# A two-layer decoder in one kernel: softmax probabilities of two attentions transposed by VectorE squares and DRAM instead of by TensorE

## The chip, the core and the metric

The kernel runs on one core of a Trainium2 chip. The core has a matrix engine (TensorE, in the profile PE, with its weight loads as PEld), a vector engine (VectorE, DVE), an activation engine (ScalarE, ACT), a general engine (GpSimd, POOL) and a queue that issues transfers (SyncE, SP). Matrix products are written to PSUM, eight banks of 128 x 512 float32; the other data are in SBUF, 128 partitions wide. The engines run side by side, each through its own list of instructions in order, and wait for each other by semaphores.

The metric is the device time of one execution in microseconds, as the median of several runs.

## What is computed

The input is x, 16 blocks of 128 tokens by 512, and a context, 16 blocks of 128 by 128. All is float32. Two layers, each with an attention, a second attention to the context, and a feed-forward part; after each of the six parts, `x = layernorm(x + part(x))`:

```python
x = _layernorm(x + _L0_attn_ref(x, ...))     # 16 heads of 32, 4 key heads, additive mask, softmax
x = _layernorm(x + _L0_xattn_ref(x, ctx, ...))  # 16 heads, keys from the context, softmax
x = _layernorm(x + _L0_ffn_ref(x, ...))      # ternary weights
x = _layernorm(x + _L1_attn_ref(x, ...))     # linear attention with decay, no softmax
x = _layernorm(x + _L1_xattn_ref(x, ctx, ...))  # 16 heads of 32, causal, softmax
x = _layernorm(x + _L1_ffn_ref(x, ...))      # mixture of 8 experts, 2 chosen, and a shared one
```

The change touches mainly the first and the fifth part. The core of both is, for each block of 128 tokens and each of 16 heads:

```python
scores = einsum("qd,kd->qk", q, k) * scale + mask    # 128 x 128
p = softmax(scores, axis=-1)
out = einsum("qk,kd->qd", p, v)                      # then all heads through an output projection
```

## The kernel before, in words

The program is written with a framework that builds the lists of the engines at compile time: a scheduler orders the instructions by priority (roughly, the order in which they are written) and by when it thinks that each is ready, and sets the semaphores. `tc.keep_in_program_order` takes an instruction out of that freedom: it stays in the written order on its engine.

The two attentions with 16 heads (called first and second attention here; lines 254 to 450 with `p1`, and 880 to 943 with `p5`) share a function, `attend`. It goes over 16 blocks `n` and 2 more turns, so that three blocks are in flight:

- **Scores** of block n: 16 small products on TensorE (L444, L931) into four PSUM banks of tag `sc`, four heads in each.
- **Softmax** in four parts `c` of four heads. `start` (L182): add the mask on VectorE into an SBUF tile `t` (L184), the row maximum on VectorE (L186), four exponentials on ScalarE with their sums (L191). `finish`, one part later: the reciprocal on VectorE (L197), a multiplication on GpSimd (L198).
- **Turn** of block n-1 (L200): the value product needs the probabilities with the keys on the partitions. `turn` transposes the four heads of a part on TensorE, by a product with the identity (L203), into a PSUM bank of tag `pt`, and VectorE copies the bank to an SBUF tile `pT` (L205).
- **Values** of block n-2: products into one `pt` bank (L450, L938), evicted by ScalarE to `oT` (L246), then `project_out` (L148, bank of tag `mm`), whose result VectorE adds to x (L149); a layer norm follows, with its last step on GpSimd (L121).
- **Preparation** of the next group of four blocks: `Share.deal` hands out, in parts between the softmax parts, the transposes of x (L127, bank `mm`, evicted by ScalarE at L128), the projections for queries, keys and values (L137 and, in the first attention, L422; bank `mm`). In the first attention the folds are dealt too: weights for the next part are multiplied together (`fold`, L283 to L307, bank `mm`), from raw weights of 1728 KB per fold, loaded by SP with two buffers (L389).

PSUM's eight banks in both attentions: 2 `mm`, 4 `sc`, 2 `pt`. A float32 product appears as two records in the profile; a transpose appears as one.

The second part (the attention to the context with wide heads, `p2`, L504 to L650) has a class `Heads` that already turns its probabilities in another way: VectorE transposes the 32 x 32 squares of a 128 x 128 matrix in place (L580), a transfer writes the result to a DRAM tile `away` (L584), and four transfers read it back with the squares moved to their places (L587). Its PSUM: 2 `mm`, 4 `sc`, 2 `av`.

The last part needs two DRAM arrays, `slots_x` and `sums`, set to zero. SP does that with two transfers of 10 MB each (L891), issued as the second attention prepares its first group, together with the loads of the shared expert's weights.

## Time and profile before

| | us |
|---|---|
| median of 3 runs | 2102.04 (2098.30 to 2102.48) |
| the profiled execution, its time | 2102.39 |
| the profiled execution, its span | 2100.6 |
| TensorE busy in the span | 2038.5 (97%) |
| VectorE busy | 853.1 (41%) |
| ScalarE busy | 625.0 (30%) |
| GpSimd busy | 646.8 (31%) |
| mean busy share of the DMA engines over the span | about 35% |
| first attention, from first score to last projection | 34.4 to 260.9 |
| second attention, likewise | 1311.5 to 1519.3 |

The span is what the engines' records cover; the execution's own time is 1.8 us longer. The profile's columns are busy times: TensorE's products are pipelined, and their ends are modelled, so a busy TensorE is not one at its peak. In the groups of instructions a line reads: line, engine, operation, output<-input, shape, count | busy us, mean ns of one | idle us of the engine before them, and what ended most of it.

### The profile page before, as it was taken

The numbers are of one execution on the slowest core, as the hardware profiler recorded it, in microseconds if no ns is written. First come the engines' busy times: TensorE is split into PE (matmuls) and PEld (weight loads), VectorE is DVE, ScalarE is ACT, GpSimd is POOL, SyncE is SP. The second block draws the span as 40 slices with busy tenths as digits, with TensorE's granted clock in tenths as the row PEclk, the third lists the DMA queues.
The fourth block names the chain that finished last, engine by engine and source line by source line (L and its number), as shares of the span: only waits on it lengthen the run. The fifth ranks groups of instructions, "written<-read, shape, count | busy, mean of one in ns | idle before, by whom it ended". The sixth has DMA issues, their size and how long they took to land. (4 is left out here: it accounts for less than half of the span.)

```text
span 2100.6 us, 25187 instructions
## 1 busy us (share of the span) xinstructions
PE 2038.5 (97%) x9221; PEld 1125.7 (54%) x9221; DVE 853.1 (41%) x1728; ACT 625.0 (30%) x2103; POOL 646.8 (31%) x674
## 2 busy tenths in 40 slices
PE   8999989999999999999999999999899999999997
PEld 5555544444444458888555444555544455545552
DVE  4667732444554243222123213777731122232324
ACT  3655532333333222222211111766632200000002
POOL 5555530111211122223223123455613212222223
PEclk9999999999999999999999999999999999999999
DMA  6001231334432220000300008600003379999974
GB/s 230 1 35 40 106 129 54 99 124 125 136 119 78 70 85 1 1 1 35 120 1 1 1 6 248 244 22 21 26 19 126 122 218 305 295 295 305 289 236 165
DMA packets 117067, 238.19 MB, mean 113 GB/s; under 512 B 28752, under 2 KB 73168, under 8 KB 110288
## 3 DMA queue, kind: packets, MB, share of 16 engines
q1 hardware_dynamic: 102048, 129.72, 19.1%
q0 software_dynamic: 13792, 105.55, 15.3%
q8 instruction: 73, 1.20, 0.2%
q10 hardware_dynamic: 1104, 1.31, 0.2%
q14 instruction: 50, 0.41, 0.1%
HBM read 172.25 MB, written 64.30 MB: 113 GB/s over the span
## 5 line engine op out<-in xcount | busy, mean ns | idle before, releaser
L198 POOL TENSOR_TENSOR p<-p,rs 128x512 f32<-128x512 f32 x192 | 200.0, 1043 | 504.8 <-DVE rs L197 500.0
L605 PE MATMUL po<-mT,cc 128*128 128x512 f32 x512 | 232.5, 602 | 3.7 <-ACT cc L598 3.7
L191 ACT ACTIVATE p<-t,nmx 128x128 f32<-128x128 f32 x512 | 198.5, 390 | 34.6 <-POOL p L198 8.8
L605 PEld LDWEIGHTS po<-mT,cc 128*128 128x128 f32 x512 | 95.5, 191 | 117.7 <-issue 107.4
L191 ACT ACTIVATE p<-sc,nmx 128x128 f32<-128x128 f32 x256 | 90.0, 372 | 113.7 <-DVE nmx L186 107.9
L546 PE MATMUL pq<-xT,wqr 128*128 128x512 f32 x256 | 117.9, 602 | 3.0 <-ACT xT L128 3.0
L114 POOL TENSOR_SCALAR ve<-mv 128x1 f32<-128x1 f32 x80 | 18.1, 226 | 324.3 <-DVE mv L112 312.3
L148 PE MATMUL po<-wo,oT 128*128 128x512 f32 x256 | 116.8, 599 | 0.4 <-ACT qkT L414 0.4
L1163 ACT ACTIVATE rsg<-rg 128x352 f32<-128x352 f32 x39 | 18.1, 463 | 331.2 <-PE rg L1158 331.2
L775 PE MATMUL pq<-xT,wq 128*128 128x512 f32 x256 | 110.9, 594 | 1.0 <-ACT xT L128 0.7
L1158 PE MATMUL rg<-ew,xsT 128*128 128x352 f32 x312 | 100.5, 465 | 11.3 <-DMA ew<-in_l1f_w_dram,which 10.6
L1179 PE MATMUL ry<-ew,ractT 128*128 128x512 f32 (+1 forms) x234 | 106.9, 592 | 0.0
L121 POOL TENSOR_SCALAR x<-x,mv,rstd 128x512 f32<-128x512 f32 x48 | 100.6, 2095 | 4.5
L1158 PE MATMUL ru<-ew,xsT 128*128 128x352 f32 x312 | 98.7, 459 | 0.0
L1129 POOL DMA_INDIRECT ew<-in_l1f_w_dram,which x39 | 38.0, 975 | 190.7 <-PE ry L1179 167.9
L191 ACT ACTIVATION_READ_ACCUMULATOR p<-t,nmx 128x1 f32 x512 | 96.2, 188 | 0.0
L698 POOL TENSOR_TENSOR hl<-ht,hh 128x512 fp32r<-128x512 f32 x44 | 60.4, 1372 | 114.9 <-ACT hh L696 114.9
L205 DVE COPY pT<-pt 128x512 f32<-128x512 f32 x128 | 86.5, 679 | 18.0 <-PE pt L203 18.0
L1189 POOL DMA_INDIRECT sums<-ry,place x39 | 62.0, 1590 | 96.2 <-DMA sums<-ry,place 43.9
L203 PEld LDWEIGHTS pt<-ident,p 128*128 128x128 f32 x512 | 59.8, 141 | 53.8 <-issue 44.8
L1041 PE MATMUL pg<-xT,sw_gu 128*128 128x512 f32 x192 | 86.5, 593 | 0.0
L186 DVE TENSOR_REDUCE nmx<-t 128x4 f32<-128x512 f32 x128 | 83.8, 675 | 0.8
(231 smaller groups left out, 3617.7 us busy)
## 6 DMA issues: line engine op xcount, KB each, us to landing
piece<-in_l0f_w_dram SPq DMA_DIRECT2D x48, 352.0 KB
away<-sq SPq DMA_DIRECT2D x32, 512.0 KB
pT<-away SPq DMA_DIRECT2D x128, 128.0 KB
raw<-in_l0x_raw_dram SPq DMA_DIRECT2D x8, 1728.0 KB
slots_x<-zero SPq DMA_DIRECT2D x1, 10023.0 KB
sums<-zero SPq DMA_DIRECT2D x1, 9984.0 KB
xs<-slots_x SPq DMA_DIRECT2D x156, 64.0 KB
sums<-x SPq DMA_DIRECT2D x16, 256.0 KB
```

Of the source, the lines that this page charges most:

```text
L121: engine.tensor_scalar(x[b], x[b], mean, rstd, ALU.subtract, ALU.mult)
L148: nc.tensor.matmul(po, lhsT=oT[:, c, :], rhs=wo[:, c, :], start=(c == 0), stop=(c == KC - 1))
L186: nc.vector.tensor_reduce(nmx, src, axis=AX.X, op=ALU.max, negate=True)
L191: nc.scalar.activation(self.p[:, j, :], src[:, j, :], AF.Exp, bias=nmx[:, j : j + 1], accum_out=self.sm[:, j : j + 1])
L198: nc.gpsimd.tensor_tensor(self.p, self.p, spread(rs, P), ALU.mult)
L205: nc.vector.tensor_copy(self.pT, pt)
L546: nc.tensor.matmul(pq, lhsT=wqr[:, k, cols], rhs=xT[:, k, :], start=(k == 0), stop=(k == KC - 1))
L605: nc.tensor.matmul(self.po, lhsT=self.cc[:, 4 * par + j, :], rhs=mT[h], start=(par == 0 and j == 0), stop=(par == 1 and j == 3),)
L775: nc.tensor.matmul(pq, lhsT=wq4[k // 2][:, k % 2, c * P : (c + 1) * P], rhs=xT[:, k, :], start=(k == 0), stop=(k == KC - 1))
L1041: nc.tensor.matmul(dst, lhsT=sw_gu[:, k, at : at + P], rhs=xTs[g][:, k, :], start=(k == 0), stop=(k == KC - 1),)
L1158: nc.tensor.matmul(dst, lhsT=self.xT[:, k, :], rhs=gu[:, k, off : off + FE], start=(k == 0), stop=(k == KC - 1),)
L1179: nc.tensor.matmul(po, lhsT=self.actT[:mw, m_, :], rhs=dn[:mw, m_, :], start=(m_ == 0), stop=(m_ == 2))
```

## The change

- The turn of the probabilities. `turn` is gone. A class `Turn` transposes the 32 x 32 squares on VectorE into a tile `sq` of half a block (two parts), sends each half to DRAM (`away`, 512 KB), and after the second half reads the block back with four transfers into one tile `pT` of 1 MB, of which there is one buffer. The last block of each attention is still turned on TensorE (`here`), through `mm` banks.
- The order. A class `Order` keeps the instructions that go through it in the written order: TensorE's, VectorE's and ScalarE's of the softmax, the squares, the eviction of `oT`, and the addition to x. `attend` is rewritten around four slots a block: values of block n-2 before slot 1, their projection in slot 2, the addition and the layer norm in slot 3, a part of the preparation in slots 0, 1 and 3; the squares of a part come two slots after its `start`. One turn fewer follows the last block.
- The masked scores are written into the tile `p` itself instead of into a tile `t`, and the exponentials are computed in place.
- PSUM. Both attentions: 2 `mm`, 5 `sc`, 1 `pt`. The second part (`p2`): 4 `mm`, 2 `sc`, 2 `av`.
- The zero fills of `slots_x` and `sums` are issued in the feed-forward stage of the first layer, before its second group.

The diff, cut to its core:

```diff
-    psum.share(mm=2, sc=4, pt=2)
+    psum.share(mm=2, sc=5, pt=1)
...
+    class Order:
+        kept = False
+        def one(self, instruction):
+            if self.kept:
+                tc.keep_in_program_order(instruction)
+        def matmul(self, *args, **kw):
+            self.one(nc.tensor.matmul(*args, **kw))
+        def transpose(self, *args):
+            self.one(nc.tensor.transpose(*args))
+    te = Order()
...
-    def project_out(oT, wo, b):
+    def project_out(oT, wo):
         po = bank("mm", [P, D], "po")
         for c in range(KC):
-            nc.tensor.matmul(po, lhsT=oT[:, c, :], rhs=wo[:, c, :], start=(c == 0), stop=(c == KC - 1))
-        nc.vector.tensor_tensor(x[b], x[b], po, ALU.add)
+            te.matmul(po, lhsT=oT[:, c, :], rhs=wo[:, c, :], start=(c == 0), stop=(c == KC - 1))
+        return po
+    def add_norm(b, po):
+        te.one(nc.vector.tensor_tensor(x[b], x[b], po, ALU.add))
         layernorm(b, nc.gpsimd)
...
             if self.mask is not None:
-                src = self.pool.tile([P, 4, P], F32, tag="t", name="t", bufs=3)
-                nc.vector.tensor_tensor(src, self.sc, bc(self.mask, 4), ALU.add)
+                src = self.p
+                te.one(nc.vector.tensor_tensor(src, self.sc, bc(self.mask, 4), ALU.add))
...
-        def turn(self):
-            pt = bank("pt", [P, 4, P], "pt")
-            for j in range(4):
-                nc.tensor.transpose(pt[:, j, :], self.p[:, j, :], ident)
-            self.pT = self.pool.tile([P, 4, P], F32, tag="pT", name="pT", bufs=4)
-            nc.vector.tensor_copy(self.pT, pt)
+    class Turn:
+        def __init__(self, pool):
+            self.pool = pool
+            self.away = dram.tile([P, 4, 2, 8 * Q], F32, tag="away", name="away", bufs=2)
+        def squares(self, c, p):
+            if c % 2 == 0:
+                self.sq = self.pool.tile([P, 4, 8, Q], F32, tag="sq", name="sq", bufs=2)
+            at = slice(c % 2 * 4, c % 2 * 4 + 4)
+            te.one(nc.vector.transpose(
+                self.sq[:, :, at, :].rearrange("p k h q -> p h k q"), p.rearrange("p h (k a) -> p h k a", a=Q)
+            ))
+            if c % 2:
+                nc.sync.dma_start(self.away[:, :, c // 2, :], self.sq.rearrange("p k h q -> p k (h q)"))
+            if c == 3:
+                self.back()
+        def here(self, ps):
+            self.pT = self.pool.tile([P, 4, 16, Q], F32, tag="pT", name="pT", bufs=1)
+            for c, p in enumerate(ps):
+                pt = bank("mm", [P, 4, P], "pt")
+                for j in range(4):
+                    te.transpose(pt[:, j, :], p[:, j, :], ident)
+                nc.vector.tensor_copy(
+                    self.pT[:, :, 4 * c : 4 * c + 4, :].rearrange("p t h q -> p h t q"),
+                    pt.rearrange("p h (t q) -> p h t q", q=Q),
+                )
+            return self
+        def back(self):
+            self.pT = self.pool.tile([P, 4, 16, Q], F32, tag="pT", name="pT", bufs=1)
+            rows = self.away.rearrange("(t a) k n f -> k a t (n f)", a=Q)
+            for k in range(4):
+                nc.sync.dma_start(self.pT[k * Q : (k + 1) * Q].rearrange("a t h q -> a t (h q)"), rows[k])
...
+        te.kept = True
+        def values(n):
+            av = bank("pt", [P, KC, P], "av")
+            held.pop(n)
+            value(av, n, turns.pop(n).pT)
+            oT = pool.tile([P, KC, P], F32, tag="oT", name="oT")
+            te.one(nc.scalar.copy(oT, av))
+            return oT
-        for n in range(NB + 2):
+        for n in range(NB + 1):
             if n % GB == 0 and n < NB:
                 share.rest()
-                share = Share(prepare(n // GB + 1), 3 * GB if n + GB < NB else 3 * GB + 6)
+                share = Share(prepare(n // GB + 1), 3 * GB if n + GB < NB else 3 * GB + 3)
             if n < NB:
                 sc = [bank("sc", [P, 4, P], "sc") for _ in range(4)]
                 score(sc, n)
                 held[n] = [Softmax(pool, sc[c], mask) for c in range(4)]
-            if n >= 2:
-                av = bank("pt", [P, KC, P], "av")
-                value(av, n - 2, [s.pT for s in held.pop(n - 2)])
-                oT = pool.tile([P, KC, P], F32, tag="oT", name="oT")
-                nc.scalar.copy(oT, av)
             for c in range(4):
+                if c == 1 and n >= 2:
+                    oT = values(n - 2)
                 if n < NB:
                     held[n][c].start()
                     late.append(held[n][c])
+                if c == 3 and n >= 2:
+                    add_norm(n - 2, po)
                 if late and (len(late) > 1 or n >= NB):
                     late.pop(0).finish()
-                if 1 <= n <= NB:
-                    held[n - 1][c].turn()
-                if c == 1 and n >= 2:
-                    project_out(oT, wo, n - 2)
+                of, part = divmod(4 * n + c - 2, 4)
+                if 0 <= of < NB - 1:
+                    if part == 0:
+                        turns[of] = Turn(pool)
+                    turns[of].squares(part, held[of][part].p)
+                if c == 2 and n >= 2:
+                    po = project_out(oT, wo)
+                elif c == 1 and n == NB:
+                    turns[NB - 1] = Turn(pool).here([h.p for h in held[NB - 1]])
                 else:
                     share.deal()
+        oT = values(NB - 1)
+        share.rest()
+        add_norm(NB - 1, project_out(oT, wo))
+        te.kept = False
...
     with tc.tile_pool(name="p2", bufs=1, reuse_waits="tile") as p2:
-        psum.share(mm=2, sc=4, av=2)
+        psum.share(mm=4, sc=2, av=2)
...
         for g in range(NG):
             hs = []
+            if g == 1:
+                zero = p3.tile([P, D + 2], F32, tag="zero", name="zero")
+                nc.gpsimd.memset(zero, 0.0)
+                for t, rows, width in ((slots_x, NT, D + 2), (sums[NB * P :], NT, D)):
+                    tc.keep_in_program_order(nc.sync.dma_start(
+                        t.rearrange("(n p) d -> p n d", p=P), zero[:, 0:width].unsqueeze(1).broadcast_to([P, rows, width])
+                    ))
...
-        psum.share(mm=2, sc=4, pt=2)
+        psum.share(mm=2, sc=5, pt=1)
```

The products of the folds, of the preparation, of the scores and of the values go through `te.matmul` and `te.transpose` now; the linear attention in between uses `add_norm(b, project_out(...))`, with the same instructions as before.

## Prediction, made before the changed kernel ran

> **What bounds the kernel now.** First the page's shares (TensorE 97% of the span, VectorE 41%), then the two 16-head attentions by themselves. The first runs from its first score at 34.43 us to its last output projection at 260.85, the second from 1311.53 to 1519.32. The view of windows gives busy us per engine in a stretch; columns are length, TensorE, weight loads, VectorE, ScalarE, GpSimd, clock, DMA share, GB/s:
>
> ```profile
> 34.43:260.85 226.42, 224.83 (x1468) 130.26 (x1469) 153.97 (x321) 133.80 (x567) 127.01 (x125) 0.98 0.12 44
> 1311.53:1519.32 207.79, 199.88 (x1613) 115.56 (x1612) 153.16 (x313) 134.08 (x571) 108.80 (x109) 1.00 0.22 82
> 1480.00:1490.00 10.00, 9.41 (x95) 6.29 (x96) 9.78 (x21) 7.43 (x36) 7.83 (x10) 1.00 0.07 26
> ```
>
> TensorE has no room in the first; in the second it is full until the last four blocks (from 1468.46), which have no next group's projections: there VectorE is the full engine, 9.78 of 10. Second, the groups of instructions (busy us, mean ns, idle before and its releaser) for the work that goes and what replaces it:
>
> ```profile
> L203 PE MATMUL pt<-ident,p 128*128 128x128 f32 x512 | 79.2, 278 | 1.7 <-DVE pT L205 1.3 <-POOL p L198 0.5
> L203 PEld LDWEIGHTS pt<-ident,p 128*128 128x128 f32 x512 | 59.8, 141 | 53.8 <-issue 44.8 <-POOL p L198 4.4 <-POOL rstd L116 1.7
> L205 DVE COPY pT<-pt 128x512 f32<-128x512 f32 x128 | 86.5, 679 | 18.0 <-PE pt L203 18.0
> L580 DVE STREAM_TRANSPOSE sq<-p 128x512 f32<-128x512 f32 x64 | 45.5, 711 | 69.9 <-POOL p L198 68.8 <-DMA pT<-away 1.2
> ```
>
> Third, the timeline of the middle stage's first blocks, which turn their probabilities by squares and DRAM already: the only rows for that trip, and for what a wait on TensorE costs beside its length (then two windows, clock next to last but two):
>
> ```profile
> 293.83 0.34 SPq L584 DMA_DIRECT2D away<-sq  x1
> 296.47 1.76 SPq L587 DMA_DIRECT2D pT<-away  x4
> 300.88 1.96 PE L593 MATMUL av<-pT,kvr 128*128 128x512 f32 x4 [1.56 <-DMA pT<-away]
> 306.58 5.76 PE L605 MATMUL po<-mT,cc 128*128 128x512 f32 x9 [3.75 <-ACT cc L598]
> ...
> 304.00:306.00 2.00, 0.00 (x0) 0.00 (x0) 1.28 (x3) 1.58 (x11) 1.04 (x1) 1.00 0.01 4
> 308.00:310.00 2.00, 2.00 (x3) 0.67 (x2) 0.71 (x1) 0.00 (x0) 0.04 (x1) 0.52 0.94 223
> ```
>
> **What is removed.** 15 of 16 blocks, 16 transposes each, two attentions: 480 of 512 on TensorE. In a full queue one costs its pitch, the 141 ns of its weight load: 67.4 us. By their share of busy time (79.2/512 = 155 ns) it is 74.2; I take 67.4. VectorE swaps a 679 ns copy for a 711 ns square transpose, 120 times: +3.8 us, of which only the last blocks of the second attention are on the path (16 x 0.032 = 0.5).
>
> **What that credit loses.**
> (1) In the second attention's last four blocks VectorE ends last, so the 64 transposes of that stretch buy nothing: 64 x 0.141 = -9.0.
> (2) The tail gains. Before, 25.1 us pass from the last score (1494.22) to the end. After: four softmax slots of VectorE at 2.2 us (0.65 + 0.65 + 0.17 + 0.71), the multiplication 1.04, four turns through PSUM at about 0.75, values 1.2, eviction 0.8, projection 3.4, and some 3 us of handovers: about 22. +3. The first attention's tail has folds to fill it: 0.
> (3) The instructions are now issued as written. Between transposes of the probabilities, always ready, the compiler had strewn the others; now the four (with the context, five) transposes of x in a group follow each other over two "mm" banks. The third waits until ScalarE has evicted the first: 0.58 us of copy behind a run of four exponentials (0.385 us pitch, 1.54 a run), against 0.56 us of cover from the second. Behind it in TensorE's queue stand the values, then everything. 0 to 3.5 us a group, six groups; I take 2: -12 (0 to -21).
> (4) Six folds, each a chain TensorE, VectorE, TensorE, VectorE, TensorE over the same two banks, with VectorE's four-instruction slots of 2.2 us ahead of its copies and a 0.86 us matmul as cover: 0 to 2 us; I take 1: -6 (0 to -12).
> (5) The DRAM trip. The first of the rows above needs 2.64 us from issue to landed for 512 KB out and 4.41 us more until TensorE reads 512 KB back, 7.05 in all. Now the last half block of 512 KB leaves in 1 KB pieces (issue of 640 pieces is 0.58 us at L844 against 0.34: 2.9 us) and 1 MB returns: 4.41 plus 1.3 to 2.6 us (512 KB at the 400 GB/s of the raw loads or the 200 of these rows): 8.6 to 9.9 us. The time for it runs from the last square (slot 1 of the next block) to the values one block later: a period of 12 us, plus scores and first share on TensorE (3.2), less scores, their latency and two VectorE slots (5.9): 9.3 us. So it just fits, and half of any excess counts, since values of block n gate the squares of n+2. Where it doesn't fit is behind the raw loads of 1728 KB, which took 5.5 us from issue (142.65) to idle DMA: in the compiled order one is issued in front of block 7's return and one in the middle of block 11's, the latter itself waiting for TensorE to end a fold. SP's queue behind it holds the remaining returns, and TensorE waits for them at once after the next scores: about 7 us there, 2 at block 7, and up to 5 at others; 0 to 14, I take -7. GpSimd's normalization (2.1 us) and bias additions (1.3) stand before multiplications that VectorE's squares wait for: up to 2.6 us in a group, hidden while VectorE has 10.4 us to do in a block of 12; without that cover it is rival 2.
> (6) The zero fills (20 MB) move from SP's queue ahead of the second attention into the FFN, where DMA share is 0.00 to 0.07 between 850 and 1000 us; at 350 GB/s they take 57 us and SP has 206 us of waiting behind them before the next weight loads. One memset on GpSimd, with 115 us of idle before its subtractions there. 0; freeing 1288 to 1342 gives at most 1.4.
> (7) PSUM of the middle stage, four banks for projections and two for scores instead of two and four: its exponentials take 4.6 us of 15 us a step, so two score banks come free in time; TensorE is idle 16.5 of 508 us there, mostly at the start and at layer norms, not for banks. 0, bounds -5 to +5.
>
> Sum: 67.4 - 0.5 - 9 + 3 - 12 - 6 - 7 = 35.9 us off the profiled execution's own 2102.39 (span 2100.6, 1.8 around it; 0.35 above the median 2102.04): **2066**. All bounds good: 74.2 - 9.5 + 3 + 1.4 + 5 = 74, 2028; all bad: 67.4 - 9.5 + 3 - 21 - 12 - 14 - 5 = 9, 2093.
>
> The Trainium skill speaks against the move: "VectorE: DVE Perf Modes", section "Rules for kernel authors", sends a 128x128 transpose to TensorE and only 32x32 ones to VectorE, with 390 and 311 ns in "The three transpose paths". The rows say 141 ns on TensorE and a quarter of 711 on VectorE; by the page's 390 ns the credit would be an estimated 187 us, more than TensorE's transposes occupy here, so the rows decide.
>
> On long waits: after the 3.75 us gap above, TensorE's clock was 0.52 for some 3.5 us, 1.7 us lost; yet it also fell to 0.50 at 42 to 46 us, after no gap over 0.4. The skill's "TensorE: Matmul & The Clock Gate" (section "What's actually happening") halves the clock after about 3.4 us of idleness; by it only block 11's wait would add such a loss, an estimated 2 us more.
>
> **Rivals.**
> 1. Waits are hidden as before: above 63 us gained, 2036 or less (2028 at best). For: TensorE waited under 2 us in 226 so far, with the same two banks. Against: that was with ready transposes between. 0.10.
> 2. VectorE in kept order paces each block: 10.4 us and 2.2 for GpSimd and ScalarE, 12.6 x 16 + 12 for the tail = 213.6 us for each attention, against 226.4 and 207.8: 7 us gained, 2095. For: VectorE was full at 1480. Against: TensorE has more to do in 12 of 16 blocks. 0.10 (a tenth of it no change).
> 3. Slower, by one mechanism, the trip: two blocks take at least 14.7 us (values of n to squares of n+2: 8.8 TensorE, 1.5 scores, 4.4 VectorE) plus the trip. With 9.3 us that is 12.0 a block; above 13.6 us it passes the old 14.15 in the first and above 11.3 the old 13.0 in the second. At 14 us: 14.35 a block, 15 x (0.2 + 1.36) = +23, 2125. For: 2 KB pieces into 32 partitions at a time, one buffer for the turned block. Against: 7.05 us measured for half the bytes. 0.13.
> 4. It doesn't matter: in-order waits eat exactly the credit, 2098 to 2106. 0.04.
>
> **How the numbers follow.** The forecast itself, 2040 to 2090 with 2066 likeliest, has the remaining 0.63. Differences under 0.2% (4.2 us, the spread of the three runs) can't be told from none. Faster: 0.63 + 0.10 + 0.09 = 0.82; same 0.05; slower 0.13. The range 2036 to 2094 leaves out rival 1 and nearly all of 3 and 4.
>
> **What would show it.** TensorE's transposes of p: 32, not 512. The first attention some 205 to 210 us long with TensorE idle for 10 to 25 of it, waiting for ScalarE (evictions of x), VectorE (banks), and the pT DMA at blocks 7 and 11; the second about 190, its last quarter unchanged. The middle stage and the MoE as long as before. I am wrong if the pT DMA leads the waits of TensorE in most blocks (rival 3), if VectorE is above 95% busy in blocks 4 to 11 (rival 2), or if TensorE stays full (rival 1).

## The result, and the profile after

| | median of 4 runs, us | profiled execution, us | span, us | granted clock |
|---|---|---|---|---|
| before | 2100.98 (2098.3 to 2102.48) | 2102.39 | 2100.6 | 0.995 |
| after | 2157.68 (2155.47 to 2164.23) | 2164.23 | 2162.4 | 0.967 |

The ratio after to before is 1.0276, 95% interval 1.0251 to 1.0302: slower by about 57 us, where 36 us less were predicted. The work that was to go is gone. TensorE makes 32 transposes of probabilities instead of 512, and VectorE's squares cost a little less than was assumed, 687 ns against 711 (groups of instructions of the changed kernel; busy us, mean ns of one, then the idle time in front of them):

```profile
L137 PE MATMUL pt<-ident,p 128*128 128x128 f32 x32 | 5.9, 338 | 0.5 <-DVE pT L248 0.4
L233 DVE STREAM_TRANSPOSE sq<-p 128x512 f32<-128x512 f32 x120 | 82.4, 687 | 19.4 <-POOL p L219 13.9 <-DMA away<-sq 5.5
L134 PE MATMUL av<-pT,v 128*32 128x128 f32 (+1 forms) x640 | 40.4, 386 | 55.7 <-DMA pT<-away 55.7
```

The last row is the one to look at: 55.7 us of TensorE's idleness stand in front of the values. The view of windows over both attentions, and then over their last four blocks with the drain (columns as in the prediction: length, busy TensorE, weight loads, VectorE, ScalarE, GpSimd, granted clock, DMA share, GB/s):

```profile
35.10:297.15 262.05, 214.65 (x1246) 108.36 (x1246) 159.41 (x322) 133.69 (x567) 126.52 (x125) 0.88 0.56 158
1341.62:1577.41 235.79, 190.57 (x1373) 95.41 (x1372) 158.28 (x313) 133.71 (x571) 107.81 (x109) 0.89 0.53 151
...
210.08:297.15 87.07, 62.07 (x373) 32.04 (x372) 45.49 (x95) 33.70 (x142) 34.42 (x35) 0.82 0.62 183
1505.11:1577.41 72.30, 47.29 (x385) 25.12 (x384) 41.56 (x83) 31.30 (x138) 35.20 (x36) 0.79 0.51 141
```

The attentions took 226.4 and 207.8 us before; they take 262.1 and 235.8, 63.6 more together. Everything else is 1.8 us shorter in this execution. VectorE has the same 159 and 158 us to do as was expected; it isn't the bound, for its share fell to 61 and 67%. TensorE, at 0.98 and 1.00 of its clock before, was granted 0.88 and 0.89.

To see what became of the credit, each attention is cut into stretches of 2 us. In each, idle time is the length less TensorE's busy time, clock loss is the busy time times one less the granted clock, and the rest is work at full clock:

| both attentions, us | length | idle | clock loss | work at full clock |
|---|---|---|---|---|
| before | 434.2 | 9.5 | 3.4 | 421.3 |
| after | 497.8 | 92.6 | 40.4 | 364.8 |

So 56.5 us of work went, and 83.1 us of idleness and 37.0 us of clock loss came. By quarters of four blocks, the first attention took 52.1, 65.3, 57.7 and 87.1 us against 48.3, 59.8, 58.8 and 59.5 before, the second 50.1, 57.9, 55.5 and 72.3 against 46.2, 55.7, 55.0 and 50.9. The two last quarters, with the drain, carry 49 of the 63.6. Three blocks from the end of the second attention (timeline of the changed kernel, TensorE; what ended a wait stands in brackets) show both losses at once:

```profile
1528.33 1.17 PE L134 MATMUL sc<-kT,qT 32*128 32x128 f32 x32
1535.36 1.93 PE L134 MATMUL av<-pT,v 128*32 128x128 f32 x32 [5.85 <-DMA pT<-away]
1538.04 6.40 PE L134 MATMUL po<-wqo,oT 128*128 128x512 f32 x8 [0.75 <-ACT oT L294]
1544.37 1.17 PE L134 MATMUL sc<-kT,qT 32*128 32x128 f32 x32
1546.43 1.08 PE L134 MATMUL av<-pT,v 128*32 128x128 f32 x32 [0.89 <-DMA pT<-away]
1550.33 5.38 PE L134 MATMUL po<-wqo,oT 128*128 128x512 f32 x8 [2.82 <-ACT oT L294]
1562.44 1.94 PE L134 MATMUL av<-pT,v 128*32 128x128 f32 x32 [6.73 <-DMA pT<-away]
...
1573.71 3.70 PE L134 MATMUL po<-wqo,oT 128*128 128x512 f32 x8 [0.76 <-ACT oT L294]
```

TensorE has nothing to do here but the scores, the values and the projection of each block. It waits 5.85 us for the turned tile, and the eight matmuls of the projection that follow take 6.40 us; the same eight take 3.70 at full clock. From 1538 to 1541 us the granted clock was 0.50. A part of a wait is thus paid again: here 2.7 us on the projection and 0.85 on the values (1.93 us against 1.08) for a wait of 5.85.

Where TensorE has other work, the change did what it was to do. One block in the middle of the second attention took 13.72 us before (scores at 1385.94 and 1399.66) and 11.95 after (1410.98 and 1422.93), with TensorE busy throughout: 1.77 us for 16 transposes, 0.11 us each.

### The profile page after: what moved, and what is told of

Same layout as the page of the kernel before. It is cut to its first block, busy times and chain, and to the rows that moved or that the text cites. A ratio compares the mean times of both kernels' runs of the same rounds, so it can differ in the third digit from the quotient of the medians.

```text
span 2162.4 us, 24334 instructions
## 1 busy us (share of the span) xinstructions
PE 2021.5 (93%) x8741; PEld 1089.3 (50%) x8741; DVE 863.5 (40%) x1728; ACT 624.4 (29%) x2103; POOL 645.3 (30%) x674
## 5 line engine op out<-in xcount | busy, mean ns | idle before, releaser
L212 ACT ACTIVATE p<-p,nmx 128x128 f32<-128x128 f32 x512 | 198.8, 391 | 116.2 <-DVE rs L218 95.0
L115 POOL TENSOR_SCALAR ve<-mv 128x1 f32<-128x1 f32 x80 | 18.1, 226 | 421.3 <-DVE mv L113 297.9
L212 ACT ACTIVATION_READ_ACCUMULATOR p<-p,nmx 128x1 f32 x512 | 96.5, 189 | 0.0
L134 PE MATMUL av<-pT,v 128*32 128x128 f32 (+1 forms) x640 | 40.4, 386 | 55.7 <-DMA pT<-away 55.7
L233 DVE STREAM_TRANSPOSE sq<-p 128x512 f32<-128x512 f32 x120 | 82.4, 687 | 19.4 <-POOL p L219 13.9
L209 DVE TENSOR_REDUCE nmx<-p 128x4 f32<-128x512 f32 x128 | 87.7, 685 | 4.3
L134 PE MATMUL pq<-xT,wr 128*128 128x512 f32 x160 | 81.4, 653 | 5.9 <-ACT xT L146 5.9
```

Source lines behind the costliest of these rows:

```text
L134: self.one(nc.tensor.matmul(*args, **kw))
L209: te.one(nc.vector.tensor_reduce(nmx, src, axis=AX.X, op=ALU.max, negate=True))
L212: te.one(nc.scalar.activation(self.p[:, j, :], src[:, j, :], AF.Exp, bias=nmx[:, j : j + 1], accum_out=self.sm[:, j : j + 1]))
L233: te.one(nc.vector.transpose(self.sq[:, :, at, :].rearrange("p k h q -> p h k q"), p.rearrange("p h (k a) -> p h k a", a=Q)))
```

## The experiments

Each run is compared with the kernel before on the same chip. "All kept" is the changed kernel with all of VectorE's and ScalarE's instructions in the two attentions kept where they are written, as those of TensorE are. A run with values from a fixed tile (e1, k1, and the three with "no DRAM trip") leaves out the product with the real probabilities: it shows times, and is no kernel to use.

| label | what it is | median, us | ratio to before, 95% interval |
|---|---|---|---|
| e1_no_wait | after; values from a fixed tile | 2194.79 | 1.0443 (1.0421 to 1.0465) |
| e2_turn_te | after; all blocks turned on TensorE | 2152.80 | 1.0242 (1.0220 to 1.0263) |
| e3_later | after; values a block later | 2179.71 | 1.0369 (1.0345 to 1.0392) |
| e5_halves | after; returns in halves | 2144.28 | 1.0191 (1.0174 to 1.0209) |
| e6_free | after; no order kept | 2170.58 | 1.0317 (1.0295 to 1.0339) |
| e7_free_halves | e5_halves; no order kept | 2258.93 | 1.0746 (1.0693 to 1.0799) |
| e4_raw_pool | after; raw loads issued by GpSimd | 2148.66 | 1.0218 (1.0201 to 1.0236) |
| e8_kept_all | all kept | 2157.50 | 1.0254 (1.0231 to 1.0277) |
| k1_no_wait | all kept; values from a fixed tile | 2149.26 | 1.0197 (1.0164 to 1.0230) |
| k3_later | all kept; values a block later | 2147.29 | 1.0195 (1.0168 to 1.0222) |
| k6_last | all kept; blocks 12 to 15 on TensorE | 2153.39 | 1.0235 (1.0203 to 1.0267) |
| k7_three | all kept; halves, raw loads, blocks 12 to 15 | 2143.62 | 1.0179 (1.0147 to 1.0212) |
| n2_halves_raw | all kept; halves (values as in after), raw loads | 2149.84 | 1.0231 (1.0211 to 1.0251) |
| n1_no_dram | all kept; no DRAM trip | 2116.07 | 1.0049 (1.0030 to 1.0069) |
| n5_no_dram_free | no DRAM trip, no order kept | 2115.45 | 1.0068 (1.0048 to 1.0087) |
| n4_no_dram_banks | all kept; no DRAM trip, 3 projection banks | 2086.20 | 0.9914 (0.9897 to 0.9931) |
| r1_banks | all kept; 3 projection banks | 2142.83 | 1.0187 (1.0166 to 1.0208) |
| r2_later_banks_raw | all kept; later, raw loads, 3 banks | 2122.67 | 1.0086 (1.0058 to 1.0114) |

### First round: the wait taken away, and the kernel slower

The trace put 55.7 us down to the returned tile, so the first theory was the prediction's rival 3, with the clock on top. The first test takes that wait away and leaves the rest, the second takes the trip away and leaves the order, the third gives the trip a block more, the fourth halves its second leg.

```
# e1_no_wait: in values(n), for blocks 0 to 14
-            value(av, n, turns.pop(n).pT)
+            turn = turns.pop(n)
+            value(av, n, turn.const if n < NB - 1 else turn.pT)   # 128x512 fixed tile
```

> Blocks 0 to 14 multiply a fixed tile by the values instead of the probabilities that came back, so the output isn't the reference's; squares, both DRAM transfers and the kept order stay. Theory (TensorE, in order, waits for the trip through DRAM, and its clock halves behind those waits): of the two attentions' 497.8 us in the changed kernel, 364.5 were work at full clock, 92.6 idle (55.7 of it put down to pT) and 40.7 lost to the clock. Without the wait for pT about 37 idle and 0 to 10 of clock remain: 400 to 415 us, the whole 2065 to 2085 us, and the granted clock back above 0.98. Rival (the kept order on two banks is what costs): the waits only move to other names; the attentions stay above 470, the whole above 2130.

```
# e2_turn_te: Turn.squares(), with psum.share(mm=2, sc=4, pt=2)
-            te.one(nc.vector.transpose(self.sq[...], p[...]))   # and its DMAs
+            pt = bank("pt", [P, 4, P], "pt")
+            for j in range(4):
+                te.transpose(pt[:, j, :], p[:, j, :], ident)
+            te.one(nc.vector.tensor_copy(self.pT[...], pt[...]))
```

> All sixteen blocks are turned on TensorE in the same slots of the kept order, with no DRAM trip; PSUM of the two attentions as before (4 score banks, 2 for turning and context). Theory (trip): the 480 transposes come back, 67 us of work, and the trip's waits go; what is left against the kernel before is the kept order alone, predicted at 18 us: 2095 to 2125, granted clock above 0.98. Rival (kept order): as slow as the changed kernel or slower, since it has the order and the transposes too: above 2150.

```
# e3_later: attend()
-        for n in range(NB + 1):
+        for n in range(NB + 2):
-                if c == 1 and n >= 2:
-                    oT = values(n - 2)
+                if c == 1 and n >= 3:
+                    oT = values(n - 3)
...
```

The projection and the add follow from n = 3 on, with two `pT` and three `away` tiles.

> Values, projection and add of a block come one block later (three behind its scores instead of two), with two turned tiles and three DRAM tiles instead of one and two; four probability tiles instead of five, and seven value tiles instead of eight in the second attention, for room. Theory (trip): it has a whole block, 9 to 13 us, more, so only the stalls behind raw loads are left; one more block of drain, about 9 us, is exposed at each end: the whole 2065 to 2095 us. Rival (bandwidth of the trip or the kept order is the bound): waits move, the whole stays above 2135.

```
# e5_halves: Turn.squares()
             if c % 2:
-                nc.sync.dma_start(self.away[:, :, c // 2, :], ...)
-            if c == 3:
-                self.back()
+                away = dram.tile([P, 4, 8 * Q], F32, tag="away", name="away", bufs=4)
+                nc.sync.dma_start(away, ...)
+                pT = self.pool.tile([P, 4, 8, Q], F32, tag=f"pT{c // 2}", name="pT", bufs=2 - c // 2)
+                rows = away.rearrange("(t a) k f -> k a t f", a=Q)
+                for k in range(4):
+                    nc.sync.dma_start(pT[k * Q : (k + 1) * Q]..., rows[k])
# value() of the second attention
-            for c in range(4):
-                for j in range(4):
+            for j in range(4):
+                for c in range(4):
```

> Each half block returns by itself, the first half two slots earlier (two tiles for it), so that behind the last square 512 KB are read back instead of 1 MB. Theory (trip too long by its second leg): 1 MB came back in 7 to 8 us from issue, half of it should take 4.4 to 5.5, a trip of 7.5 to 8.8 us instead of 10.3, below the 9.3 there is: half to two thirds of the 55.7 us of waits and of the 37 us of clock go: 2095 to 2120 us. Rival (the write, not the read, is what is late): below 10 us gained, above 2145.

Measured: 2194.8, 2152.8, 2179.7 and 2144.3. The theory said 2065 to 2085, 2095 to 2125, 2065 to 2095 and 2095 to 2120, so all four missed (e2_turn_te and the two slower ones fell on their rivals' sides), and the kernels with the wait removed (e1_no_wait) or given more time (e3_later) were slower than the one that had it. In e1_no_wait, TensorE's waits had moved to the eviction of the context by ScalarE (38.6 us; the second row stands in the last block, whose turned tile waited for the returns that nobody read any more):

```profile
PE po L134 <- ACT oT L300: 38.6, 13, 6.0
PE pt L137 <- DVE pT L251: 25.7, 2, 13.8
```

Its timeline shows why (block of the first attention, all engines; only the rows of VectorE, TensorE and ScalarE that matter):

```profile
115.31 0.69 DVE L209 TENSOR_REDUCE nmx<-p 128x4 f32<-128x512 f32 x1
...
117.27 1.06 PE L134 MATMUL av<-cpT,v 128*32 128x512 f32 x8
117.38 0.69 ACT L492 ACTIVATE qkT<-pq,br 128x512 f32<-128x512 f32 x1 [3.56 <-PE pq L134]
...
118.94 0.40 ACT L212 ACTIVATE p<-p,nmx 128x128 f32<-128x128 f32 x1
```

The row maxima were there at 116.0, but ScalarE stood 3.56 us in front of the eviction of a projection that TensorE had not finished, with the exponentials behind it. That eviction is one of the instructions which the change does not keep in order: the compiler places them by its own durations, and it placed them anew in e1_no_wait and in e3_later, where ScalarE's order in the first attention differs from the changed kernel's. So these two compare two things at once. The lesson for the next round was to fix the order of everything before taking something away.

e2_turn_te tells less than it was meant to. Its TensorE waits (30.4 us) for GpSimd's normalization in front of the transposes, which in these slots follow it at once; so it shows that this order costs some 50 us with the transposes in it, not what it costs without them.

### Second round: the order undone, and the order completed

```
# e6_free (after) and e7_free_halves (e5_halves): attend()
-        te.kept = True
# e8_kept_all: transpose_x()
-        nc.scalar.copy(xT[:, :, at : at + P], tr)
+        te.one(nc.scalar.copy(xT[:, :, at : at + P], tr))
# e4_raw_pool: folds()
-                nc.sync.dma_start(raw, a["l0x_raw"][i]...)
+                nc.gpsimd.dma_start(raw, a["l0x_raw"][i]...)
```

In e8_kept_all, the same is done to the evictions of `qkT`, `v`, `ctT`, `kT`, `qT`, of the folds (`cT`, `ch`, `mT`, `wqr`) and of `here()`, and to the layer norm's statistics.

> Nothing of the two attentions is kept in written order; squares, DRAM and PSUM stay as in the changed kernel. Theory now (the kept order ties TensorE, VectorE and ScalarE to each other, so that each late result, the DRAM trip's among them, stops the next instructions although others are ready): without it most of the 57 us less work on TensorE shows: 2070 to 2110 us. Rival (the DRAM trip alone is too long, whatever the order): 2140 us or more, with the pT DMA still leading TensorE's waits above 40 us.

> Return in halves as in the run with half returns, and no kept order. Theory (order first, trip second): the two gains add, some 13 us below the run with no kept order: 2055 to 2100 us. Rival (only the trip counts): about 2144, as with half returns alone.

> Order kept as in the changed kernel, and the instructions of VectorE and ScalarE that it left to the compiler (evictions of turned x, of projections, of folds, the statistics) are kept where they are written, too. Theory A (the half that is left free is placed by wrong durations, so that an eviction waits on ScalarE in front of exponentials): idle of TensorE in the attentions falls below 60 from 92.6 us, 2105 to 2135 us. Theory B (any fixed order across the engines costs, since each eviction now stands behind four exponentials or a VectorE slot): 2155 us or more.

> The raw weight loads of the folds are issued by GpSimd instead of standing in the queue of the returns. Predicted for them was 7 us at block 11, 2 at block 7, up to 5 elsewhere; 11.0 was seen at block 11. Theory (they are a small part of the loss): 8 to 20 us better than the changed kernel, 2138 to 2150. Rival (they are the main part, with the clock behind them): 2120 or less. If the queue plays no part because the loads share the DMA engines' bandwidth with the returns: within 6 us of 2157.

Measured: 2170.6, 2258.9, 2157.5 and 2148.7. Undoing the kept order gains nothing (1.0317 against 1.0276), and with half returns it loses 117 us by the ratios, so the theory of the first two expectations fell: giving the order up is no cure. The rival of e6_free had the time right and its sign wrong, for the turned tile held TensorE up for 22.0 us there, behind the eviction of the context with 28.0. Why half returns lose so much without the order stays open. Completing it changes nothing that can be told either (1.0254 against 1.0276, intervals overlap): the number of theory B. Whether B's reason holds is not shown: the runs with no order are no faster, yet the fourth round finds an eviction that stands behind four exponentials. The worth of e8_kept_all is as a base: from here on, TensorE, VectorE and ScalarE issue the same instructions in the same order with and without the thing under test. The raw loads out of the returns' queue gain about 12 us by the ratios (1.0276 less 1.0218, of 2104), inside the first expectation.

### Third round: the wait, with the order fixed

The edits are those of e1_no_wait and e3_later on top of e8_kept_all; k6_last and k7_three are:

```
# k6_last: attend(), FIRST = 12
                 if c == 1 and n >= 2:
                     oT = values(n - 2)
+                if c == 1 and FIRST < n < NB:
+                    turns[n - 1] = Turn(pool).here([h.p for h in held[n - 1]])
-                if 0 <= of < NB - 1:
+                if 0 <= of < FIRST:
# k7_three: k6_last, with the edits of e5_halves and e4_raw_pool
```

> Blocks 0 to 14 multiply a fixed tile by the values instead of the returned probabilities (so the output isn't the reference's), now on top of the kernel in which all of TensorE, VectorE and ScalarE is kept, so that these three engines issue exactly the same instructions in the same order with and without the wait; the DRAM trips still run. Theory (the trip, waited for in order, is the largest single loss): the 45.8 us of TensorE's waits on pT and about half of the clock's 40 us go: 2080 to 2110 us against 2157.5. Rival (the first run without the wait was right, and the order costs the same with any data): 2150 us or more.

> Values, projection and add one block later, again with all three engines kept in written order. Theory (trip; the first run with later values lost to evictions that the compiler had placed anew): the trip is hidden in all blocks but the drain, and the whole stands 5 to 20 us above the run without the wait: 2095 to 2125. Rival: as without that order, 2170 or more, ScalarE's eviction of the context leading TensorE's waits.

> Blocks 12 to 14 of each attention are turned on TensorE too (all four parts together after the values, as block 15 is), the others by squares and DRAM; order all kept. Theory (the loss sits where TensorE has no or little other work: the last quarters, 87.1 and 72.3 us against 59.5 and 50.9 before): they come down to 60 to 70 and 50 to 60, the whole to 2115 to 2135 us. Rival (the loss is even over the blocks, or four times sixteen transposes in one place cost what the trip costs): above 2145 us.

> All three together: half returns, raw loads issued by GpSimd, blocks 12 to 15 turned on TensorE; order all kept. Theory: the gains of the single runs add (13 us, 9 us and 22 to 42 us off 2157.5): 2093 to 2113 us, level with the kernel before. Rival (they remove the same waits): 2115 to 2140 us.

Measured: 2149.3, 2147.3, 2153.4 and 2143.6. All four theories missed; k6_last fell on its rival's side, k1_no_wait and k3_later between the two, and k7_three above both. Taking the wait of the values away gains 12 us by the ratios, a block more for the trip as much, and turning the last blocks on TensorE in one piece nothing that can be told (their quarters took 81.3 and 69.7 us, against 86.7 and 70.3 in e8_kept_all). Yet the order was now the same, and 45.8 us of waits were gone. Where they went is in the trace of k1_no_wait. First TensorE's waits, then SP's queue and VectorE in the last quarter of the first attention:

```profile
PE pt L137 <- DVE pT L251: 19.3, 2, 14.4
PE po L134 <- ACT oT L300: 18.0, 8, 3.8
...
PE po L134 <- DVE cT L365: 8.9, 1, 8.9
```

```profile
202.22 15.12 SPq L467 DMA_DIRECT2D raw<-in_l0x_raw_dram  x2
217.43 1.71 SPq L240 DMA_DIRECT2D away<-sq  x2
...
226.78 0.71 DVE L236 STREAM_TRANSPOSE sq<-p 128x512 f32<-128x512 f32 x1 [7.21 <-DMA away<-sq]
```

SP's queue stood at a raw load from 202.2 to 217.3, because that load's tile is read by a fold that TensorE had not done (14.1 us of it are put down to the fold's products, `pg`). The half blocks on their way out queued behind it, and from 217.4 they moved beside its 1728 KB, until 226.7. VectorE has two square tiles; the third square waited 7.21 us for one to be written out, and everything in VectorE's order waited with it, the copy `cT` of a fold among it, for which TensorE then stood 8.9 us. The 19.3 us at the last blocks are the same kind: `here()` uses the buffer that the returns still fill. The trip has more ends than the one that waits longest, and a kernel that removes one of them shows the next.

### Fourth round: no trip at all

```
# n1_no_dram: k1_no_wait, and in Turn.squares()
-            if c % 2:
-                nc.sync.dma_start(self.away[:, :, c // 2, :], ...)
-            if c == 3:
-                self.back()
# n4_no_dram_banks: n1_no_dram with psum.share(mm=3, sc=4, pt=1) in both attentions
# n5_no_dram_free: n1_no_dram without te.kept = True
# n2_halves_raw: e8_kept_all with half returns (value() as in after) and raw loads by GpSimd
```

> The kernel with all of TensorE, VectorE and ScalarE kept, without the DRAM trip: the square transposes are made and go nowhere, blocks 0 to 14 multiply a fixed tile by the values (so the output isn't the reference's). The three engines issue the same instructions in the same order. Theory (the trip, both legs: the values' wait, the square tiles that are not free, the queue it shares with weight loads): idle of TensorE falls from 95 to 40 to 55 us and the clock's loss from 38 to 10 to 20: 2075 to 2115 us. Rival (the kept order loses it by itself): above 2130 us, with VectorE's and ScalarE's evictions leading the waits.

> The run without the trip, with three banks for projections and four for scores instead of two and five. Theory (the chains of turned x and of folds over two banks are the rest, predicted at 18 us): 10 to 20 us below the run without the trip. Rival (four score banks hold up the next block's scores, or the rest is the softmax's own chain): no gain, within 5 us of it or slower.

> Neither trip nor kept order: what the removed transposes are worth at all, with the compiler's own order. Theory (the credit of 67 us was right, less 9 us in the last blocks): 2035 to 2060 us. Rival (without transposes between, the compiler's order loses as much as the kept one): above 2085 us.

> Correct kernel: all order kept, half returns with the values' matmuls in the changed kernel's order (the earlier run with half returns had them turned round in the second attention and worked 25 us longer there), raw loads issued by GpSimd. Theory: 13 us of the halves, 9 of the raw loads and the 25 add: 2105 to 2125 us. Rival (the longer work hid waits that now show): 2130 to 2145 us.

Measured: 2116.1, 2086.2, 2115.5 and 2149.8. n1_no_dram came out 1 us above its theory's range, n4_no_dram_banks gained more than its theory said, n5_no_dram_free fell on its rival's side, and n2_halves_raw above both. The windows of both attentions without the trip, and then with the third bank too:

```profile
35.19:267.82 232.63, 207.34 (x1246) 105.22 (x1246) 159.02 (x322) 133.18 (x567) 126.54 (x125) 0.94 0.11 42
1313.14:1531.46 218.32, 183.44 (x1373) 91.80 (x1372) 157.70 (x313) 133.68 (x571) 107.84 (x109) 0.92 0.05 19
```

```profile
35.80:259.57 223.77, 202.75 (x1246) 105.18 (x1246) 159.00 (x322) 133.09 (x567) 126.44 (x125) 0.95 0.12 42
1302.74:1507.54 204.80, 177.45 (x1375) 90.00 (x1375) 157.68 (x313) 132.98 (x571) 107.81 (x109) 0.94 0.06 20
```

Cut into 2 us stretches as above:

| both attentions, us | length | idle | clock loss | work at full clock |
|---|---|---|---|---|
| before | 434.2 | 9.5 | 3.4 | 421.3 |
| e8_kept_all | 496.6 | 95.4 | 37.6 | 363.5 |
| k1_no_wait | 490.8 | 87.4 | 40.0 | 363.5 |
| n1_no_dram | 451.0 | 60.2 | 25.6 | 365.1 |
| n5_no_dram_free | 452.0 | 45.7 | 22.3 | 384.0 |
| n4_no_dram_banks | 428.6 | 48.3 | 20.7 | 359.6 |

This prices two parts of the loss. The trip as a whole costs 45.6 us in the attentions (496.6 to 451.0), 43 of the run by the ratios; 32 of the 45.6 lie in the two last quarters (86.7 to 64.4, and 70.3 to 60.3). A third projection bank, paid with the fifth score bank, is worth 22 us in the attentions and 28 by the ratios. Even without any trip, and so with 56 us less work (37 in the free order), the kernel is no faster than before, kept or free (1.0049 and 1.0068): idleness and clock loss, 12.9 us before, are 85.8 and 68.0. In n1_no_dram, the last blocks of the second attention show such a gap bare (TensorE and ScalarE):

```profile
1504.78 1.17 PE L134 MATMUL sc<-kT,qT 32*128 32x128 f32 x32
1505.88 1.08 PE L134 MATMUL av<-cpT,v 128*32 128x128 f32 x32
...
1508.57 0.40 ACT L212 ACTIVATE p<-p,nmx 128x128 f32<-128x128 f32 x1 [2.52 <-DVE rs L218]
...
1510.12 0.56 ACT L295 COPY oT<-av 128x512 f32<-128x512 f32 x1
...
1510.74 6.59 PE L134 MATMUL po<-wqo,oT 128*128 128x512 f32 x8 [3.78 <-ACT oT L295]
```

The values are done at 1507.0, but ScalarE evicts them behind the four exponentials of slot 0, which wait for VectorE (its mask and maximum of the scores just made end at 1508.48). With no projections to do in between, TensorE idles 3.78 us and runs the next 6.59 at about half clock. The kernel before, at the same place:

```profile
1469.57 1.08 PE L938 MATMUL av<-pT,v 128*32 128x128 f32 x32
1470.58 0.66 PE L203 MATMUL pt<-ident,p 128*128 128x128 f32 x4
1470.77 0.59 ACT L246 COPY oT<-av 128x512 f32<-128x512 f32 x1 [1.61 <-PE av L938]
...
1472.07 3.60 PE L148 MATMUL po<-wqo,oT 128*128 128x512 f32 x8
```

There ScalarE evicted the values at once, and the projection began 1.4 us after they were done, with eight transposes in between. So the transposes hid at most 1.4 us; the other 2.4 of the 3.78 come with the later place of the eviction. Whether that place or VectorE's work ahead of the mask (it is busy for 3.51 of the 3.78 us) sets the last quarters without a trip is not shown: moving the eviction in front of the exponentials was not tried.

n2_halves_raw took 2149.8 us, against 2144.3 of e5_halves. The rival's reason, that the turned-round values of e5_halves, 2.46 us a block instead of 1.08, had filled time that is waited away in n2_halves_raw, would fit, but it was not tested by itself: e5_halves leaves the evictions to the compiler, and n2_halves_raw keeps them.

### Fifth round: a correct kernel with both

> A correct kernel: all order kept, trip as in the changed kernel, three banks for projections and four for scores. Theory (bank chains and trip are separate losses): 25 to 35 us off 2157.5, 2122 to 2133 us. Rival (with the trip the bank chains stand in its shadow): within 10 us of 2157.

> A correct kernel: values one block later, raw loads issued by GpSimd, three banks for projections and four for scores, order all kept. Theory: 2147 of the later values, less 30 for the bank and 9 for the loads: 2100 to 2115 us, beside the kernel before, which the run without any trip (2086) bounds from below. Rival (the longer drain and the order's own chains remain): 2120 or more.

r1_banks is e8_kept_all with `psum.share(mm=3, sc=4, pt=1)` in both attentions, r2_later_banks_raw the same on k3_later with the raw loads of e4_raw_pool. Measured: 2142.8 and 2122.7. With the trip in place the third bank gains 14 us by the ratios, half of the 28 without it, and TensorE's wait for the returned tile grows from 45.8 to 62.1 us: so the other half seems to have gone into the trip's shadow, between the two expectations. r2_later_banks_raw is the fastest correct kernel of this family, but still 0.86% (0.58 to 1.14) above the kernel before, over its expectation and on its rival's side. In these runs nothing correct beat the kernel before.

## Why the prediction was wrong

Three steps failed: the trip of term (5), priced at 7 us, cost 45.6; the last four blocks of the second attention, which term (1) took as unchanged, lost 21.4; and the clock, left out of the sum, lost 37.0. These overlap (the trip's 45.6 hold its waits and the clock lost behind them, in the last blocks too) and don't add up. Their common ground is that the terms were priced over whole attentions instead of where TensorE has least to do.

**The credit**, 67.4 us, measured 56.5 (work at full clock, 421.3 to 364.8). In a full block a transpose was worth 0.11 us and not the 0.141 of its weight load. This error of 11 us is small beside the three.

**(5), the trip**, was given 7 us and cost 45.6. Its length was mis-sized first: 8.6 to 9.9 us were predicted, and the steps were 3.3 us from the issue of the last half to the issue of its return and 7.0 from there to the values where nothing was in the way (1416.83, 1420.12; 1390.97, 1397.93), so 10.3 us, and 5.1 and 7.9 in an early block (84.54, 89.62, 97.47), so 12.9. The first of these, in the rows of SP and TensorE:

```profile
1416.83 0.52 SPq L237 DMA_DIRECT2D away<-sq  x1
1420.12 1.73 SPq L258 DMA_DIRECT2D pT<-away  x4
1427.16 1.08 PE L134 MATMUL av<-pT,v 128*32 128x128 f32 x32 [1.14 <-DMA pT<-away]
```

That is over the 9.3 us available by the prediction's own count, and TensorE waited for the turned tile in 15 of the 30 blocks that made the trip. The collision at block 11 was foreseen at 7 and took 11.0. What was not priced at all are the trip's other ends, which k1_no_wait laid bare: VectorE's two square tiles, and SP's queue, where a raw load that waits for a fold stops the outgoing halves too. The prediction followed what is queued behind the returns and not what is queued behind the writes.

**(1), the last four blocks of the second attention**, was the step that failed in kind. "VectorE ends last" was read from the profile before, where these blocks took 8.6 us each (1468.46 to 1494.22 for three), and the quarter was taken to stay as it was. By rival 3's own formula the trip allows no less than 12.0 us a block even at 9.3 us; this was set against the averages of 14.15 and 13.0, never against the 8.6 of these, where it costs 3.4 us a block at once. Measured, the quarter took 72.3 us instead of 50.9, and 60.3 with no trip at all, so 12 of the 21.4 us are the trip's. The other 9.4 come with the late eviction of the context, a cause that the trace suggests and no run isolates. **(2)**, the drain, was to be 22 us from the last score: it took 33.0, and 26.7 without the trip.

**(3) and (4), the bank chains**, were the right mechanism: 18 us predicted, and the third bank gives 22 in the attentions once the trip is out of the way, clock loss included. The waits for evicted x and context were still 10.6, 6.4 and 5.9 us in n1_no_dram.

**The clock** was named and then left out of the sum, 2 us. It lost 37.0. The Trainium skill, "TensorE: Matmul & The Clock Gate" (section "What's actually happening"), says that the clock is halved after about 3.4 us of idleness. The trace agrees for the long wait (0.50 after the 5.85 us) and shows it after a shorter one too: behind the 2.82 us in front of the projection at 1550.33, the granted clock was 0.51 from 1550.3 to 1552.3 us. The prediction counted one such wait, at block 11; the timeline above has three in the last blocks of the second attention alone. Without the trip 25.6 us of it remain, behind the other waits.

**(6) and (7)** held: between the attentions the kernel is 6.2 us shorter (1050.7 to 1044.5 us), at the edge of the bounds of 1.4 and 5 us; behind the second attention it is 3.7 us longer, where the prediction had no change. Two readings there were a little off, without weight in the sum: between 850 and 1000 us the DMA share is 0.00 to 0.01 until 990 and 0.71 after it, and TensorE is idle for 15.2 and not 16.5 of the 508 us.

**Rival 3** had the right sign and the sign by which it was to be known, the pT DMA leading TensorE's waits. It explains 43 to 46 of the 113 us lost (56.5 of work gone, and still 57 slower), and its time, 2125 us, was too low. Rival 1 and rival 2 are out: TensorE idles 92.6 us and VectorE is below 70%. What of the loss stays open: with neither the trip nor the two-bank limit, 38.8 us of idleness and 17.3 of clock loss over the kernel before remain (n4_no_dram_banks), nearly half of the 120 us that the changed kernel has over it. The waits named there are the context's eviction (19.2 us) and evicted x and context inputs (20.8); that these are the whole of it is argued, not shown.

## What to carry to other kernels

Removing work from the busiest engine buys less than that work's time where the engine then waits instead: here 56 us of it, and even without the trip no gain until a third projection bank was added (18 us). Before removing it, look for the latency that will show, in the stretch with the least other work, and price that stretch by itself against its own old pace. A trip through DRAM has to be priced at each of its ends, the source's buffers and the queue that carries it as much as the reader that waits. To measure one wait, first fix the order of all engines, and then remove the whole transfer and not one of its waits.

## What the hardware showed that was not expected

- Waits cost TensorE nearly half as much again in clock: 92.6 us of idleness in the changed kernel's attentions came with 40.4 us of clock loss, 60.2 in n1_no_dram with 25.6. In the rows above, a projection of 3.70 us took 5.38 to 6.59 behind waits of 2.82 to 5.85 us.
- The order of small matmuls inside the values counts. In the second attention each head writes 32 rows of the result; 32 matmuls that go round the four groups of rows take 1.08 us, and the same 32 with each group's eight in a row 2.46 (e5_halves below, after that the changed kernel, both from the timeline):

```profile
1410.75 2.46 PE L134 MATMUL av<-pT,v 128*32 128x128 f32 x32
1424.08 2.46 PE L134 MATMUL av<-pT,v 128*32 128x128 f32 x32
```

```profile
1414.00 1.08 PE L134 MATMUL av<-pT,v 128*32 128x128 f32 x32
```

The Trainium skill has the ground of this in "TensorE: Matmul & The Clock Gate", section "Part 3: Packing small matmuls — row/col tiling": small products in different columns of the array run beside each other, 2.38 times faster for three. Here it is 2.46 to 1.08, 2.28 times, for four, and only where products of different groups follow each other.
